# A two-layer decoder: order of the first loads and of the first values, and the place of the causal attention's first preparation

## The chip, the cores and the metric

The kernel runs on one core of one Trainium2 chip. The metric is device time in microseconds (us) of one execution, the median of several runs. Engines are named as in the profile: PE (TensorE matmul), PEld (TensorE weight load), DVE (VectorE), ACT (ScalarE), POOL (GpSimd) and SP (SyncE, which here issues most of the DMAs; ACT's queue issues a few).

## What is computed

A decoder of two layers on x of shape (4, 512, 256), everything in float32. Each of the six parts adds its result to x after a layer norm. Cut to what matters here:

```python
x = x + L0_attn(layernorm(x))     # 16 heads of 64, rope, kerple bias, a small network over heads
x = x + L0_xattn(layernorm(x), ctx_1024)
x = x + L0_ffn(layernorm(x))      # attention with 8 heads, 5 experts for values and outputs
x = x + L1_attn(layernorm(x))     # causal, 16 heads of 16, rope
x = x + L1_xattn(layernorm(x), ctx_1024, mask)
x = x + L1_ffn(layernorm(x))      # 32 routed experts and 2 shared ones

def L0_attn(x):                   # per batch
    q, k, v = split(x @ w_qkv); q, k = rope(q), rope(k)
    scores = q @ k.T / 8
    kerple = -softplus(log_p) * log1p(softplus(log_a) * distance)
    hidden = gelu(concat(scores, kerple, over heads) @ w1 + b1)
    scores = scores + kerple + hidden @ w2 + b2
    return softmax(causal(scores)) @ v @ w_o
```

The small network mixes the 16 heads at each pair of positions, so it needs all heads of a score block side by side.

## The kernel before

Partitions hold 128 tokens or 128 channels. x stays in SBUF for the whole kernel as 16 tiles of 128 tokens, four per batch (`TB` = 4, `NT` = 16).

**The first attention** (`l0_attn`) works on blocks (b, ib): batch b, 128 query rows ib, and the ib + 1 blocks of keys that the causal mask leaves. `turned(b, side, g)` projects a group of four heads of queries (side 0) or keys (side 1): it loads 256 KB of weights (tile `wqk`, three buffers), projects two halves on PE (L125), multiplies each with cosine and sine on DVE (L212, L213) into `rope_c` and `rope_s`, of one buffer each, and subtracts and adds on POOL (L214, L215) into `qk`. `scores(b, ib, g0, ng, on_act)` multiplies queries and keys of `ng` groups (L235), scales the result out of PSUM on ACT (L247, for the rows in `on_act`) or DVE (L245) into a ring `sc` of six buffers, and stores it from SP to DRAM (L248); the heads come to lie side by side there. `fetch(b, ib)` reads a block back as `st` (L260). Then for 16 groups of rows g: `hidden` (L269 on PE, L271 on DVE, gelu L272 on ACT, L273 on POOL) and `refined` (L281 on PE, L287 on DVE); and, for 16 groups, `weights` (the exponential, L301 on ACT), followed by the division. `values` projects one 128 x 512 piece of v (eight units per batch, PE L125, out by ACT L223).

Work of other blocks is put between these groups by hand: the list `beside(b, ib)` goes beside the network, `beside_weights(b, ib)` beside the exponentials; there about 70% of the list is placed and the rest (`left`) goes beside the first three groups of the next block. For block (0,0) `beside` holds the scores of (0,1) and (0,2), and `beside_weights` the values of batch 0 and the statistics of batch 1. The order of PE, ACT, DVE and POOL is the order of the program (`manual_schedule`); each is a queue, and an instruction that waits holds all behind it. SP's order is the scheduler's.

Ahead of that, before: x is loaded whole (2 MB) as the first load of SP's queue; `wv` and `wo` (1 MB each) go out on ACT's queue; SP loads `cs` (512 KB) and the small weights, then the distances. The kerple term `ker` is computed in a buffer of `rope_c`, so the norm, which writes `rope_c` too, comes after `hk`, the network's share of `ker` (L179, L180). Then follow the norm of batch 0, its transposes, all eight `turned`, all scores of block (0,0) in one call, and the fetch.

**The ffn of layer 0** (`l0_ffn`) walks 64 steps: step s handles pair of heads s mod 4 of token tile t = s // 4 with scores, row maximum and exponential (L1344, L1351, L1352), transposes (L1363), the output (L1380), and later `divide`, `weigh` (five products with the expert mask on POOL, L1408, in tile `mix`, three buffers), `total`, `experts` and `rows`, which add to x (L131). `at(step, f)` puts a call at a step. `spread(b)` puts the preparation of batch b beside batch b - 1; the last batch (steps 48 to 63) has nothing of that kind beside it.

**The causal attention** (`causal`, inside `l1_heads`) follows. For its first batch, before: weights and rope table are loaded, the norm is taken, four transposes (`tokens`), four projections (`turned`, two sides of two halves, L1121 on DVE), the sums on POOL and stores to a DRAM tile `way` (`store`, L1131, L1132), memsets of the padded buffers `m4`, `kT`, `qT`, `v` on POOL (`preset`, L790 to L795), and the reads of `way` back into `qT` and `kT` (`fetch`, L1138), all ahead of the first score matmul (L579); the value projections come at the first steps.

Of the kernel before, what the change touches and what calls it, by code (L numbers as in the profile page):

```python
# [134 lines left out]
def l0_attn(k, a):  # L135
# [7 lines left out]
    with ExitStack() as ctx:  # L143
# [7 lines left out]
        wv = load(k, wp, a, "l0a_wv", eng=nc.scalar)  # L151
        cs = load(k, wp, a, "l0a_cs")
        w1s, w1k, w2, b1, pab = (load(k, wp, a, "l0a_" + n) for n in ("w1s", "w1k", "w2", "b1", "pab"))
        wo = load(k, wp, a, "l0a_wo", eng=nc.scalar)


        sp = t_(wp, [P, 2], F32, "sp")
        nc.vector.tensor_scalar(sp, pab[:, 0:2], -1.0, None, ALU.mult)
        sq = t_(wp, [P, 2], F32, "sq")
        nc.vector.tensor_tensor(sq, sp, pab[:, 0:2], ALU.min)  # L160
        nc.scalar.activation(sq, sq, AF.Exp)
        nc.scalar.activation(sq, sq, AF.Ln, bias=k.one[:, 0:1])
        nc.vector.scalar_tensor_tensor(sp, pab[:, 0:2], 0.0, sq, ALU.max, ALU.add)
        ker = t_(work, [P, 2, S], F32, "rope_c", 1)[:, 0, :]
        nc.sync.dma_start(out=ker, in_=a["l0a_dist"])
        nc.scalar.activation(ker, ker, AF.Ln, bias=k.one[:, 0:1], scale=sp[:, 1:2])
        nc.vector.tensor_scalar(ker, ker, sp[:, 0:1], -1.0, ALU.mult, ALU.mult)

        kerm = t_(wp, [P, S], F32, "kerm")
        nc.vector.tensor_scalar(kerm, ker, pab[:, 2:3], None, ALU.add)  # L170
        ahead = t_(wp, [P, 8], F32, "ahead")
        nc.sync.dma_start(out=ahead, in_=a["l0a_ahead"])
        nc.vector.tensor_tensor(kerm[:, 504:512], kerm[:, 504:512], ahead, ALU.add)

        hk = t_(wp, [P, 2, S], F32, "hk")
        for half in range(2):
            rows = slice(half * 64, half * 64 + 64)
            ps = k.ps()
            nc.tensor.matmul(ps, lhsT=w1k[rows], rhs=ker[rows], start=True, stop=True)  # L179
            nc.scalar.activation(hk[:, half], ps, AF.Identity, bias=b1[:, 0:1])  # L180
# [230 lines left out]
        def beside(b, ib):  # L411

            if ib == 0:
                before = output_list(b - 1, 3)
                return before + (score_list(0, 1) + score_list(0, 2) if b == 0 else [])
            if ib == 1:
                return mixed(mixed(score_list(b, 3), output_list(b, 0)), norms.pop(b + 1, []))
            if ib == 2:
                return output_list(b, 1)
            out = output_list(b, 2)  # L420
            return out[:6] + score_list(b + 1, 0) + out[6:]

        def beside_weights(b, ib):

            if ib == 0:
                return mixed(value_list(b), norm_list(b + 1) if b + 1 < B else [])
# [3 lines left out]

        ET = mybir.EngineType
        with k.tc.manual_schedule(engines={ET.PE, ET.Activation, ET.DVE, ET.Pool}):
            for _, f in norm_list(0) + norms.pop(0) + turned_list(0, range(4)) + score_list(0, 0):
                f()
            fetch(0, 0)
            fill = []
# [409 lines left out]
def cross(k, a, pre, wp, work, bufs, preset, masked=None):  # L846
    nc = k.nc
    if True:
        rest = {}

        def fetch(*names):
            for n in names:
                if n == "keep_kT":
                    of = t_(wp, [P, 2560], F32, "held").bitcast(BF16)[:, : SC // P * S]
# [14 lines left out]
        def last():  # L869
            for n in ("wo", "bo") + ("bv",) * (masked is not None):  # L870
                rest[n] = load(k, wp, a, pre + n)
            rest["wv"] = load(k, wp, a, pre + "wv", tag="l1_wv" if masked else None)
# [10 lines left out]
        def prep(b, m):  # L883
# [8 lines left out]
            def turned(i):  # L892
                if i == 0:
                    xs["T"] = t_(work, [P, 2, S], F32, "xnT", 1)
# [35 lines left out]
            def queries(c, n):  # L930
                if n == c == 0:

                    xs["q"] = t_(work, [P, 2, S], F32, "ln_xn", 1)
# [16 lines left out]
            norm = fs(norm_units(k, work, b, xs, on_act=start), 0.4)  # L950
# [136 lines left out]

def causal(k, a, wp, work, bufs, preset):
    nc = k.nc
    if True:  # L1090
        wv = load(k, wp, a, "l1a_wv", tag="l1_wv")
        wo = load(k, wp, a, "l1a_wo")

        both = t_(wp, [P, 2560], F32, "held")
        wqk = both[:, :1024].rearrange("p (i s n) -> p i s n", i=2, s=2)
        tab = both[:, 1024:].rearrange("p (i n) -> p i n", i=3)
        nc.sync.dma_start(out=wqk, in_=a["l1a_wqk"])
        nc.sync.dma_start(out=tab, in_=a["l1a_tab"])

        def prep(b, m):  # L1100
            qT, kT, v = bufs[b % 2]
            xs = {}

            def tokens(i):
                if i == 0:
                    xs["T"] = t_(work, [P, 2, S], F32, "xnT", 1)
                transposed(k, xs["xn"], xs["T"], i)

            def turned(side, half):
                if half == 0:  # L1110

                    xs["s", side] = t_(work, [P, 2, 2, S], F32, ("stage", "cT")[side], 1)
                st = xs["s", side]
                ps = k.ps()
                proj(
                    k, ps, lambda i: wqk[:, i, side, half * P : (half + 1) * P],
                    lambda i: xs["T"][:, i, :],
                )

                for own, n in (0, 0), (1, 1 + half):  # L1120
                    nc.vector.scalar_tensor_tensor(  # L1121
                        st[:, own, half ^ own], ps, (0.25, 1.0)[side], tab[:, n], ALU.mult, ALU.mult
                    )

            def store(side):
                st = xs["s", side]
# [773 lines left out]
```

## Time and profile before

The median of three runs is 3678.42 us (3677.25 to 3681.02). The profile is of one more execution.

| | us |
|---|---|
| profiled execution, its time | 3683.43 |
| its span in the profile | 3681.7 |
| PE busy | 3418.3 |
| DVE busy | 2152.5 |
| ACT busy | 1536.3 |
| POOL busy | 941.9 |
| first statistics of x (L48) | at 11.22 |
| first rope product (L212) | at 28.96 |
| first network matmul of block (0,0) (L269) | at 79.97 |
| first network matmul of block (0,1) | at 125.39 |
| end of the ffn's last addition to x | at 1977.39 |
| first causal score matmul (L579) | at 2014.22 |

An engine's busy time is the sum over its instructions; a DMA that is issued is not counted for the issuing engine. The chain of waits is followed back from the last instruction: each row is what released the next. In rows by stretch the granted clock is the share of full speed at which PE was let run. Idle time on an engine that nobody waits for costs nothing, so the weak stretches of PE are what to look at, and in each the wait that ends last.

### The profile page before, as it was taken

To read this page: it belongs to the slowest core of one execution; us is meant where nothing else is said; L and a number is where in the kernel's file an instruction comes from. 1 tells how busy PE (TensorE), PEld (TensorE's weight loads), DVE (VectorE), ACT (ScalarE), POOL (GpSimd) and SP (SyncE) were. 2 spreads that over 40 slices of the span, in tenths; PEclk is the share of its full clock that TensorE was granted. 3 is DMA by queue.
4 is the path that set the end of the run, shared out by engine and by line. 5 is a ranking of instruction groups with operands and counts; after the bars stand their busy time and mean duration, and the time that the engine had idled before them with its cause. 6 is when DMAs were issued, how large, how long until landed. Compare 5 with 4: busy or idle time off the path is not lost.

```text
span 3681.7 us, 51748 instructions
## 1 busy us (share of the span) xinstructions
PE 3418.3 (93%) x19152; PEld 1591.2 (43%) x19152; DVE 2152.5 (58%) x4822; ACT 1536.3 (42%) x3329; POOL 941.9 (26%) x1167
## 2 busy tenths in 40 slices
PE   5999999997799999979995999999999999999999
PEld 3445454453443333345553444333333244444444
DVE  3575676755477666467783677888888622122211
ACT  1545555455445555634442344444445511111111
POOL 2342433423311012036673322000000012222222
PEclk8999999998899999979997899999999999999999
DMA  3423323141120111000002121010010032111111
GB/s 122 161 81 113 115 97 111 63 149 58 42 44 21 30 33 46 1 21 1 1 1 63 29 58 44 12 29 13 18 18 1 16 133 94 50 52 49 52 52 43
DMA packets 118877, 196.58 MB, mean 53 GB/s; under 512 B 12384, under 2 KB 62048, under 8 KB 116448
## 3 DMA queue, kind: packets, MB, share of 16 engines
q1 hardware_dynamic: 118080, 190.65, 17.1%
q8 instruction: 151, 2.47, 0.3%
q10 hardware_dynamic: 544, 2.62, 0.2%
q14 instruction: 102, 0.84, 0.1%
HBM read 128.74 MB, written 51.90 MB: 49 GB/s over the span
## 4 chain that ended last, share of the span: by engine, by line
PE 78%; DVE 9%; issue 4%; POOL 4%; ACT 2%; DMA 2%; SPq 0%; ACTq 0%; DVEq 0%; POOLq 0%
PE ps L572 15%; PE big L125 10%; PE ps L125 10%; PE av L647 8%; PE ps L579 6%; PE acc L1568 5%; PE hp L269 4%; PE ps L281 3%; PE ps L330 2%; PE ps L348 2%; PE ps L235 2%; PE ps L586 2%; PE ps L362 2%; DVE hd L271 1%; PE ps L1344 1%
## 5 line engine op out<-in xcount | busy, mean ns | idle before, releaser
L591 ACT ACTIVATE pT<-ps 128x512 f32<-128x512 f32 (+3 forms) x1280 | 649.9, 565 | 614.0 <-PE ps L579 335.3
L579 PE MATMUL ps<-kT,qT 32*128 32x512 f32 (+3 forms) x2560 | 791.3, 611 | 34.5 <-DMA kT<-way 20.9
L572 PE MATMUL ps<-q,kT 32*128 32x512 f32 (+3 forms) x2560 | 682.1, 606 | 0.7 <-DVE mx L615 0.6
L125 PE MATMUL big<-xnT,w 128*128 128x512 f32 x1088 | 492.5, 596 | 0.0
L1556 DVE TENSOR_TENSOR gu<-big,silu 128x512 f32<-128x512 f32 x136 | 94.0, 691 | 572.3 <-ACT silu L1554 572.1
L612 DVE TENSOR_REDUCE mx<-ps 128x1 f32<-128x512 f32 x512 | 326.6, 685 | 163.8 <-PE ps L579 163.6
L615 DVE CUSTOM_DVE_ANT_0 junk<-ps,mask_q 128x512 bf16<-128x512 f32 x512 | 353.0, 689 | 92.9 <-PE ps L572 25.6
L572 PEld LDWEIGHTS ps<-q,kT 32*128 32x128 f32 x2560 | 212.8, 183 | 337.8 <-ACT pT L591 117.9
L1554 ACT ACTIVATE silu<-big 128x512 f32<-128x512 f32 x136 | 81.2, 597 | 619.4 <-PE big L125 619.4
L647 PE MATMUL av<-pT,v 128*32 128x512 f32 (+3 forms) x2560 | 323.1, 574 | 0.5 <-ACT un L655 0.4
L125 PEld LDWEIGHTS big<-xnT,w 128*128 128x128 f32 x1088 | 208.1, 191 | 262.5 <-issue 262.5
L272 ACT ACTIVATE hd<-hd 128x16 f32<-128x16 f32 (+51 forms) x256 | 162.8, 636 | 351.9 <-DVE hd L271 351.8
L273 POOL TENSOR_TENSOR st<-st,kerm 128x8 f32<-128x8 f32 (+51 forms) x256 | 190.4, 745 | 460.6 <-PE hp L269 398.1
L579 PEld LDWEIGHTS ps<-kT,qT 32*128 32x128 f32 x2560 | 255.5, 185 | 118.4 <-issue 47.3
L1560 POOL TENSOR_TENSOR gu<-gu,cb 128x512 f32<-128x512 f32 x128 | 163.5, 1277 | 552.6 <-DVE gu L1556 508.1
L1568 PE MATMUL acc<-gu,w 128*128 128x512 f32 x544 | 257.9, 597 | 8.0 <-POOL gu L1560 8.0
L53 POOL TENSOR_TENSOR ln_rstd<-ln_rstd,mhalf 128x4 f32<-128x4 f32 x24 | 24.5, 1022 | 900.1 <-DVE ln_rstd L52 893.9
L269 PE MATMUL hp<-st,l0a_w1s 64*128 64x104 f32 (+26 forms) x1024 | 193.2, 455 | 55.3 <-DVE hd L271 46.2
L271 DVE TENSOR_TENSOR hd<-hp,hk 128x16 f32<-128x16 f32 (+51 forms) x256 | 178.4, 697 | 84.5 <-PE hp L269 78.5
L281 PE MATMUL ps<-hd,l0a_w 128*64 128x104 f32 (+26 forms) x1024 | 170.0, 411 | 32.2 <-ACT hd L272 25.9
L615 DVE CUSTOM_DVE_ANT_0 junk<-ps,ahead 128x256 bf16<-128x256 f32 (+3 forms) x256 | 125.5, 490 | 84.6 <-PE ps L579 58.4
L1352 ACT ACTIVATE pr<-ps,nmax 128x512 f32<-128x512 f32 x128 | 87.0, 686 | 192.3 <-DVE nmax L1351 192.1
(241 smaller groups left out, 4989.2 us busy)
## 6 DMA issues: line engine op xcount, KB each, us to landing
cb<-comb SPq DMA_DIRECT2D x128, 256.0 KB
scr<-sc SPq DMA_DIRECT2D x112, 256.0 KB
st<-scr SPq DMA_DIRECT2D x16, 1024.0 KB
w<-in_l1f_w SPq DMA_DIRECT2D x34, 384.0 KB
scr<-sc SPq DMA_DIRECT2D x64, 192.0 KB
st<-scr SPq DMA_DIRECT2D x16, 768.0 KB
wqk<-in_l0a_wqk SPq DMA_DIRECT2D x32, 256.0 KB
st<-scr SPq DMA_DIRECT2D x16, 512.0 KB
```

Source lines behind the costliest of these rows:

```text
L125: k.nc.tensor.matmul(out, lhsT=lhsT(c), rhs=rhs(c), start=start and c == 0, stop=stop and c == 1)
L269: nc.tensor.matmul(hp[:, half, :n], lhsT=w1s[rows], rhs=s[rows, :n], start=True, stop=True)
L271: nc.vector.tensor_tensor(hd[:, :, :n], hp[:, :, :n], hk[:, :, S - n :], ALU.add)
L273: nc.gpsimd.tensor_tensor(s[:, :n], s[:, :n], kerm[:, S - n :], ALU.add)
L281: nc.tensor.matmul(rp[half * 64 : half * 64 + 64, :n], lhsT=w2, rhs=hd[:, half, :n], start=True, stop=True,)
L572: nc.tensor.matmul(pa[h][:, :w], lhsT=kT[rows, c, kb * P : (kb + 1) * P], rhs=q2s[g][rows, q0:], start=True, stop=not on_pe(g, h), tile_po ...
L579: nc.tensor.matmul(pb[r][:, :uw], lhsT=uqT[rows, uc, qb * P : (qb + 1) * P], rhs=ukT[rows, uc, kh * 512 : kh * 512 + uw], start=True, stop ...
L591: nc.scalar.activation(pT[:, h, :w], pa[h][:, :w], AF.Exp)
L612: nc.vector.tensor_reduce(to, pb[r], AX.X, ALU.max)
L615: nc.vector.tensor_tensor_reduce(out=junk[:, :uw], in0=pb[r][:, :uw], in1=mask, scale=1.0, scalar=-3.0e38, op0=ALU.add, op1=ALU.max, accum ...
L647: nc.tensor.matmul(avs[g][h * 32 : h * 32 + 32, q0:], lhsT=v[:, kb, (c * 4 + h) * 32 : (c * 4 + h) * 32 + 32], rhs=pT[:, h, : S - q0], sta ...
L1568: nc.tensor.matmul(accs[b][:, n, :], lhsT=w[e][:, 512 + n * P : 512 + (n + 1) * P], rhs=g, start=e == experts[0], stop=e == experts[-1],)
```

## The change

**Loads.** x is loaded in two pieces, batch 0 first on SP, the rest later on ACT's queue. `pab`, the distances, `w1k` and `b1` go on ACT's queue at the start, `cs`, `w1s`, `w2` and `ahead` on SP's. `wv` is loaded on ACT's queue after the fifth and sixth `turned`, x's rest and `wo` after the last scores of block (0,0).

**Front.** `ker` has a buffer of the ring `sc`. The norm and the transposes come first, then `from_kerple` (the same instructions as before, in a function), then the eight `turned` in four pairs, `made_of_kerple` after the first, and the scores of block (0,0) one group of heads at a time, one pair behind, each evicted by ACT alone (16 stores in place of 4). The eight value units of batch 0 come right after the fetch of block (0,0). The scores of (0,2) leave the list beside the network of block (0,0) and take the place of the values beside its exponentials.

**Joint.** A pool `pre` is open over the ffn and layer 1. A class `Rotated` holds the causal part's first loads, norm, transposes, projections and stores. `l0_ffn` calls it at step 44 and puts the norm at steps 48 to 52, transposes at 54 and 55, queries at 57 to 59, keys at 60 to 62, the staging in two buffers of `mix`; here the norm is on DVE and not on ACT. For batch 0 `causal` keeps the memsets, the reads of `way` and the values, in this order, ahead of the first scores. In `weigh` of the last two tiles two of the five products go to DVE.

```diff
-        wv = load(k, wp, a, "l0a_wv", eng=nc.scalar)
-        cs = load(k, wp, a, "l0a_cs")
-        w1s, w1k, w2, b1, pab = (load(k, wp, a, "l0a_" + n) for n in ("w1s", "w1k", "w2", "b1", "pab"))
-        wo = load(k, wp, a, "l0a_wo", eng=nc.scalar)
...
-        ker = t_(work, [P, 2, S], F32, "rope_c", 1)[:, 0, :]
-        nc.sync.dma_start(out=ker, in_=a["l0a_dist"])
...
+        ker = t_(work, [P, S], F32, "sc", 6)
+        pab = load(k, wp, a, "l0a_pab", eng=nc.scalar)
+        nc.scalar.dma_start(out=ker, in_=a["l0a_dist"])
+        w1k, b1 = (load(k, wp, a, "l0a_" + n, eng=nc.scalar) for n in ("w1k", "b1"))
+        cs, w1s, w2, ahead = (load(k, wp, a, "l0a_" + n) for n in ("cs", "w1s", "w2", "ahead"))
+        wv, wo = (t_(wp, a["l0a_" + n].shape, F32, "l0a_" + n) for n in ("wv", "wo"))
...
             if ib == 0:
-                before = output_list(b - 1, 3)
-                return before + (score_list(0, 1) + score_list(0, 2) if b == 0 else [])
+                return output_list(b - 1, 3) if b else score_list(0, 1)
...
             if ib == 0:
-                return mixed(value_list(b), norm_list(b + 1) if b + 1 < B else [])
+                there = value_list(b) if b else score_list(0, 2)
+                return mixed(there, norm_list(b + 1) if b + 1 < B else [])
...
-            for _, f in norm_list(0) + norms.pop(0) + turned_list(0, range(4)) + score_list(0, 0):
+            for _, f in norm_list(0) + norms.pop(0):
                 f()
+            from_kerple()
+            for g in range(5):
+                if g < 4:
+                    for _, f in turned_list(0, (g,)):
+                        f()
+                if g == 0:
+                    made_of_kerple()
+                if g == 2:
+                    nc.scalar.dma_start(out=wv, in_=a["l0a_wv"])
+                if g:
+                    scores(0, 0, g - 1, 1, (0, 1, 2, 3))
+            nc.scalar.dma_start(out=k.x[:, TB:], in_=a["x"][:, TB:])
+            nc.scalar.dma_start(out=wo, in_=a["l0a_wo"])
             fetch(0, 0)
+            for _, f in value_list(0):
+                f()
...
+class Rotated:
+    def __init__(self, k, a):
...
+        self.wv = load(k, k.pre, a, "l1a_wv", tag="l1_wv")
...
+        nc.sync.dma_start(out=self.wqk, in_=a["l1a_wqk"])
+        nc.sync.dma_start(out=self.tab, in_=a["l1a_tab"])
+    def units(self, b, stage):
...
+        norm = norm_units(k, k.pre, b, xs)
+        return norm, [lambda i=i: tokens(i) for i in range(TB)], sides
...
             if b == 0:
                 chains = [
-                    (0, 0, norm + turns + fs([lambda: preset(0, 0, S)]) + sides + got),
-                    (0, 2, vs),
+                    (0, 0, fs([lambda: preset(0, 0, S)]) + got + vs),
...
             for e in range(FE):
-                nc.gpsimd.tensor_tensor(
+                eng = nc.vector if t >= NT - 2 and e % 2 else nc.gpsimd
+                eng.tensor_tensor(
...
+            def ahead():
+                k.rotated = Rotated(k, a)
+                norm, turns, sides = k.rotated.units(
+                    0, lambda side: t_(work, [P, 2560], F32, "mix", 3)[:, : 4 * S].rearrange(
+                        "p (o h n) -> p o h n", o=2, h=2
+                    ),
+                )
+                for i, u in enumerate(norm):
+                    at(n - 16 + i // 2, u)
+                for i, u in enumerate(turns):
+                    at(n - 10 + i // 2, u)
+                for i, u in enumerate(sides[0]):
+                    at(n - 7 + i, u)
+                for i, u in enumerate(sides[1]):
+                    at(n - 4 + i, u)
+            at(n - 20, ahead)
...
-        nc.sync.dma_start(out=k.x, in_=a["x"])
+        nc.sync.dma_start(out=k.x[:, 0:TB], in_=a["x"][:, 0:TB])
```

The functions `tokens`, `turned` and `store` are moved from `causal` into `Rotated` unchanged but for the tile that they stage in, which the caller gives. The second cross-attention takes some tiles from `pre` too, with the same instructions.

## The prediction, made before the changed kernel was run

> **What bounds the kernel now.** I read the page first (section 1, then the 40 slices), then the busy time by stretch around the two weak slices, then the chain of waits there, and last the rows in order of time.
>
> ```profile
> span 3681.7 us, 51748 instructions
> PE 3418.3 (93%) x19152; PEld 1591.2 (43%) x19152; DVE 2152.5 (58%) x4822; ACT 1536.3 (42%) x3329; POOL 941.9 (26%) x1167
> PE   5999999997799999979995999999999999999999
> PEclk8999999998899999979997899999999999999999
> ```
>
> PE is busy nearly everywhere, so a cut pays only where PE starves: slice 0 (0 to 92 us) and the two slices around 2000 us. The diff works at exactly these two places. I call them the front and the joint.
>
> ```profile
> 25.00:70.00 45.00, 35.08 (x120) 16.86 (x120) 19.97 (x32) 0.20 (x1) 19.77 (x16) 0.88 0.15 47
> 70.00:80.00 10.00, 0.84 (x10) 0.55 (x10) 1.29 (x2) 2.37 (x3) 0.12 (x1) 0.50 0.51 155
> 80.00:116.60 36.60, 29.25 (x256) 18.50 (x256) 13.64 (x59) 11.22 (x29) 6.07 (x23) 0.72 0.62 206
> 116.60:125.40 8.80, 8.80 (x23) 3.73 (x22) 3.11 (x15) 8.24 (x35) 1.82 (x12) 1.00 0.13 47
> ...
> 1900.00:1954.00 54.00, 53.56 (x465) 35.93 (x464) 39.37 (x63) 35.27 (x93) 18.43 (x18) 1.00 0.00 1
> 1954.00:1977.00 23.00, 12.53 (x84) 8.21 (x82) 7.35 (x12) 3.79 (x11) 10.24 (x10) 0.79 0.00 1
> 1977.00:2014.20 37.20, 11.03 (x24) 4.78 (x25) 7.87 (x19) 3.23 (x8) 15.88 (x15) 0.64 0.46 116
> ```
>
> Columns: stretch, length, busy time of PE, weight load, DVE, ACT, POOL, granted clock, DMA share, GB/s. Front: rope (25 to 70), a wait of 10 us for scores to go to DRAM and back, then block (0,0): its network (80 to 116.6) and its weights (to 125.4). Joint: the ffn's last batch fills PE; its tail leaves PE half idle; then 37.2 us pass before the first causal score.
>
> ```profile
> 42.22 1.26 POOL qk L214
> 43.48 1.23 POOL qk L215
> 44.71 0.02 issue
> 44.74 0.69 DVE rope_c L212
> ...
> 77.11 2.81 DMA st<-scr
> ...
> 98.14 5.69 DMA scr<-sc
> ...
> 116.68 8.78 PE ps L125 x20
> ```
> ```profile
> 1964.15 5.12 POOL mix L1408 x5
> ...
> 1984.43 8.88 PE ps L125 x16
> ...
> 1997.20 9.53 DMA way<-cT
> ...
> 2008.09 6.00 DMA kT<-way
> ```
>
> Chain rows are start, length, what. Rope is a serial loop of DVE and POOL over one pair of buffers: the DVE rows start every 5.08 us (39.66, 44.74, 49.82), eight times. PE only follows.
>
> **Front, term by term.** *Start.* Before, the first stats wait for all of x (11.22), SP's queue then stands until 15.25 behind the big loads, and DVE's norm comes after the kerple work (22.36); rope begins at 28.96. After, a quarter of x comes first. No row shows a 512 KB load alone. The third wqk load (256 KB) lands 3.5 us after its issue (16.58 to 20.09) and the other 256 KB cost 0.8 us at 322 GB/s, the mean of the first 16 us; with the 0.80 of the issue and some company (dist, cs) I take 5.5. Bounds: 4.5, and 11.2 if the order changes nothing. From there: stats and root 3.5 (11.22 to 14.75), norm, transposes and four copies 2.9. ACT then does the kerple chain that DVE's queue now has before the first rope product: two table loads of 1.28, Exp 0.2, Ln 0.29 and 0.81, and on DVE 0.16 + 0.48 + 0.48 + 0.17: 5.2. Rope starts at 17.1. The projections are ready earlier (5.5 + 3.5 + 2.9 + 3.7 cold = 15.6), so kerple decides. **-11.8.**
>
> *Rope.* Still 8 x 5.08. The 16 scores evictions are all on ACT, idle there (0.20 us busy), so DVE loses nothing. SP issues 16 stores in place of 4, some 0.6 each, and a wqk load queued behind four of them (2.4 us) lands late for its projection twice or so: **+1.5** (0 to 4).
>
> *Gap.* From the last POOL row (70.12) to the first network matmul (79.97) PE waits 9.85. The eight value units, 32 matmul instructions at 8.78/20 = 14.0, now stand there, behind 1.6 of scores: 15.8, **+6.0**. They cover the wait for st. But x's rest and wo, 2.5 MB, start on ACT's queue just then, beside the last store and 1 MB of st: 3.75 MB at 297 GB/s (the first 20 us) is 12.6, plus about 3 to start and land: level with the values. Bounds: +5 and +11.
>
> Here a rule speaks against the change: the Trainium skill, DMA: Bandwidth & Descriptors, "Issuing engines are not separate DMA queues", says that transfers from any issuing engine share 16 DMA engines and interleave. The trace agrees at the start, where x, 2 MB, needs 10.4 us beside 2 MB on ACT's queue. If st had priority the gap would be +6.0, and by the rule it is +6 to +8.
>
> *Network of block (0,0).* Four calls of scores(0,2) leave it: on the chain 2.80 + 2.87 + 2.87 and the 5.69 of waiting for an sc buffer, so 36.3 - 14.2 = 22.1. From below: 16 steps of about 1.2 (0.9 at 80.92, 1.5 at 91.22) and two calls of scores(0,1) at 2.4: 24. I take 24: **-12.3** (22 to 30).
>
> The same stretch ran at a granted clock of 0.72. The skill's TensorE: Matmul & The Clock Gate, Part 1, gives half rate after an idle window of about 3.4 us and full rate after a busy one; the 0.50 in the gap agrees. By it the values keep PE warm and 29.25 us of PE work would shrink by up to 8; my 24 uses rows that are partly warm, so the sum has some of that.
>
> *Weights of block (0,0).* Values (8.78) leave, but ACT set that stage's length (8.24 of 8.80), so nothing is saved. Three of the four scores(0,2) calls come in: 2.3 MB through six sc buffers, while DVE and ACT, in order, hold weights and divisions behind a full ring. At 206 GB/s (80 to 116.6) that is 11.4; with a table load 13: **+3.9** (0 to +9). *Opening of (0,1).* Three value units leave (3 x 1.91), one scores call stays: **-3** (-4 to +3).
>
> Front: -11.8 + 1.5 + 6.0 - 12.3 + 3.9 - 3 = **-15.7**.
>
> **Joint.** *Weigh.* POOL's five products take 5.12, twice on the chain (1954.20, 1964.15). Three stay on POOL (3.07), two go beside them to DVE (0.69 each): 2 x 2.05 = **-4.1** (0 if POOL and DVE slow each other, -4.1).
>
> *Work moved into the last batch.* PE: 16 projection instructions at 0.43 (their spacing from 29 to 50 us) = 6.9, transposes 8 x 0.14 (1.09 for eight of L1363) = 1.1, so 8.0. PE has no slack (53.56 of 54), so it all counts. DVE gets 4 x 0.57 + 0.17 + 4 x 0.35 + 8 x 0.65 = 9.1 on 39.4 of 54; POOL 1.0 + 5.0 on 18.4; ACT four copies. Their cover is their slack; scores wait for DVE's maximum, so some shows: **+9.5** (0 to 20). SP is idle in the ffn, so the loads and the four stores delay nobody. The stores' 9.5 us end before the ring gives their mix buffer to weigh, five steps (17 us) on. The new pool only moves tiles to other addresses: nothing.
>
> *Gap.* What remains after the ffn's last matmul: m4, kT and qT memsets 0.99 + 1.81 + 1.80 on POOL, then eight fetches on SP (1.74 + 2.51), the last landing 6.0 after its issue: 4.6 + 3.7 + 6.0 = 14.3 in place of 37.2: **-22.9**. Before, the first load there is issued at 1977.01, at the end of the ffn's last matmul, so I let the memsets wait for it; if they need not, the gap is about 6 (-31); if the fetches collide with mask loads, 19 (-18). Values run in that wait and no longer between the first scores: 3.13 + 1.99, part of it then idle anyway: **-2** (-4 to 0).
>
> Joint: -4.1 + 9.5 - 22.9 - 2 = **-19.5**.
>
> **Sum.** -35. The profiled execution took 3683.4 (span 3681.7), 0.14% over the median of 3678.4; the same cut from the median gives **3643** (3648 for a profiled execution).
>
> **Rivals.** *The front gives most of it back* (0.17): scores(0,2) are bound by stores wherever they stand. For: 5.69 on the chain, 0.62 DMA share. Against: 8.8 us at a share of 0.13 just after. Network 30, weights 18, start as summed: -11.8 + 1.5 + 8 - 6.3 + 9 + 3 = +3.4, so 3678 - 19.5 + 3 = 3662. *The last batch pays double* (0.09), +20: 3654. *Memsets are not held* (0.08): 3643 - 8 = 3635. *It doesn't do what it says* (0.02): x's quarter lands no earlier, as the queues share engines: +5.7, 3649. *Slower* (0.03): the adds put DVE and POOL in front of scores, max and Exp in each of the last 16 steps, so the batch runs at the pace of the earlier ones, which carry the next batch's preparation and take 96.0 (POOL 63, DVE 74 busy). With 8.0 of PE and 5.0 of POOL adds on top: 109 for 54, +55 in place of +9.5: 3678 - 44.7 + 55 = 3689. It decides once that batch passes 54 + 44.7 = 98.7. Against: the earlier batches' POOL has 28 us of products, the moved work 6.
>
> **How the numbers follow.** Forecast 0.61, 3632 to 3655 on its own. The range 3626 to 3664 takes in all but the ends of the first rival and the slower one; front bounds of some 10 each way and joint bounds of some 11 add to about 15 when independent, a little more on the late side. A measurement of this kernel can tell about 0.2%, or 7 us: faster 0.94, same 0.03, slower 0.03.
>
> **What would show it.** First stats near 5.5, rope's first product near 17, its last POOL row near 60, first network matmul near 75 with 14 us of value projections before it, and block (0,1)'s first near 110 (125.4 before). Last batch's 54 at 62 to 65; weigh at 3.1 on POOL twice; first causal score some 14 after the ffn's last matmul and about 35 earlier in all than 2014. It is wrong if waits on sc fill the weights stage, if projections wait in the rope for wqk, or if PE idles in the last batch.

## The result and the profile after

The changed kernel takes 3660.07 us (median, 3658.52 to 3660.62) against 3679.51 us (3677.25 to 3681.02) for the kernel before on the same chip: a ratio of 0.9947, 95% interval 0.9930 to 0.9964, so 19.4 us less. The direction was as forecast and the time lies inside the range; the size was too large by 17 us (3643): the time lies outside the main forecast's own range (3632 to 3655, chance 0.61) and near the 3662 of its first rival. The two profiled executions, which the sum was made on, took 3683.43 and 3658.52: 24.9 us less, where the terms said 35.2.

The page of the changed kernel, its first lines and two of its rows of 40 slices:

```profile
span 3656.8 us, 51742 instructions
PE 3419.3 (94%) x19089; PEld 1595.7 (44%) x19152; DVE 2156.1 (59%) x4827; ACT 1537.0 (42%) x3339; POOL 940.2 (26%) x1163
PE   7899899997799999979997999999999999999999
PEclk8899999998899999989997899999999999999999
```

PE's busy time did not fall (3419.3 against 3418.3, with 63 matmul records missing here; the same kernel run again, with all records, has 3426.8), so all of the gain is PE idle time that went. Slice 0 rose from 5 to 7 tenths. By stretch, with the same columns as before (stretch, length, PE, weight load, DVE, ACT, POOL, granted clock, DMA share, GB/s):

```profile
25.00:58.30 33.30, 23.52 (x97) 10.48 (x95) 14.99 (x24) 2.36 (x12) 16.36 (x14) 0.85 0.34 103
58.30:74.40 16.10, 16.09 (x42) 7.10 (x42) 0.00 (x0) 4.89 (x11) 0.00 (x0) 0.89 0.70 234
74.40:100.20 25.80, 21.87 (x191) 15.45 (x190) 10.38 (x51) 9.07 (x23) 5.80 (x21) 0.67 0.27 89
100.20:106.00 5.80, 4.19 (x38) 2.06 (x39) 3.21 (x12) 5.79 (x27) 1.86 (x12) 1.00 0.49 157
106.00:126.50 20.50, 15.61 (x82) 7.46 (x82) 9.97 (x34) 9.85 (x30) 3.28 (x10) 0.67 0.66 231
1890.00:1946.30 56.30, 56.30 (x437) 35.36 (x435) 41.26 (x67) 31.71 (x85) 21.47 (x20) 1.00 0.05 13
1946.30:1969.80 23.50, 14.90 (x107) 10.12 (x101) 13.95 (x20) 6.01 (x16) 7.98 (x6) 0.86 0.05 18
1969.80:1984.50 14.70, 5.24 (x17) 4.10 (x17) 0.41 (x1) 1.49 (x4) 9.91 (x10) 0.73 0.73 98
```

The gap after the rope is full of values (16.09 of 16.10), the network of block (0,0) takes 25.8 in place of 36.3, and the joint's empty stretch 14.7 in place of 37.2. The stretch that did not shrink is 106 to 126.5, the opening of block (0,1): PE works 15.6 of 20.5, and at a clock of 0.67.

The start, in DVE's rows in order of time (start, length, line, operation; in brackets the idle time before and what ended it):

```profile
5.91 0.43 DVE L48 BATCH_NORM_STATS2 ln_st<-x 128x6 f32<-128x256 f32 x1 [5.91 <-DMA x<-in_x]
...
16.22 0.17 DVE L421 TENSOR_TENSOR kerm<-kerm,l0a_ahead 128x8 f32<-128x8 f32 x1
16.30 0.69 DVE L191 TENSOR_TENSOR rope_c<-ps,l0a_cs 128x512 f32<-128x512 f32 x1
```

The quarter of x lands at 5.91 (11.22 before), and the kerple chain is what the first rope product waits for, as worked out: 16.30 in place of 28.96. At the joint, the chain of waits (start, length, what):

```profile
1958.10 4.00 POOL mix L1449 x3
...
1966.53 3.24 PE ps L1477 x6
1969.77 0.03 POOLq L804
1969.80 0.07 issue
1969.87 0.99 POOL m L804 x2
1970.86 1.74 POOL kT L805
1972.60 1.76 POOL qT L807
...
1977.42 6.87 DMA kT<-way
1984.29 0.20 issue
1984.48 4.55 PE ps L593 x15
```

The memsets (L804 to L807) start when the ffn's last matmul ends, then come the fetches, whose last transfer takes 6.87; the first causal score stands at 1984.48. Nothing of the norm, the projections, or the store to `way` is left in the chain.

To place gains and losses, it helps to have marks that every kernel here has: the start of POOL's reciprocal root (L53) of each layer norm. Five of them are used below: batch 1's norm in the first attention, the last norm of the ffn, the second and the third of the causal attention, and the time from its third to its fourth.

| | batch 1 | ffn, last | causal, 2nd | causal, 3rd | 3rd to 4th | end (span) |
|---|---|---|---|---|---|---|
| before | 127.1 | 1814.3 | 2028.6 | 2065.8 | 73.9 | 3681.7 |
| after | 116.8 | 1799.6 | 1995.4 | 2034.0 | 80.9 | 3656.8 |
| difference | -10.3 | -14.7 | -33.2 | -31.8 | +7.0 | -24.9 |

So the change was ahead by 31.8 at the third causal norm, and 7 us of that were lost in the next 81 us, in code that the diff does not touch. The windows there, of before, then of after:

```profile
2066.00:2084.00 18.00, 16.23 (x89) 7.33 (x89) 9.55 (x38) 6.07 (x14) 4.02 (x9) 0.99 0.22 39
2084.00:2094.00 10.00, 10.00 (x52) 5.33 (x52) 4.13 (x16) 3.06 (x11) 0.81 (x2) 0.51 0.00 1
2094.00:2140.00 46.00, 45.61 (x352) 22.06 (x344) 33.94 (x118) 21.56 (x55) 14.06 (x27) 1.00 0.19 47
```
```profile
2034.00:2042.00 8.00, 6.72 (x43) 3.56 (x44) 5.95 (x25) 2.19 (x6) 2.58 (x5) 0.98 0.49 85
2042.00:2068.00 26.00, 24.78 (x86) 9.98 (x84) 6.68 (x25) 6.59 (x17) 2.44 (x6) 0.50 0.00 1
2068.00:2115.00 47.00, 46.80 (x361) 22.76 (x360) 34.84 (x121) 21.92 (x56) 13.88 (x27) 0.99 0.20 46
```

Both run a while at a granted clock of one half there: 10 us before, 26 after.

The marks scatter between executions of the same code. Eight profiles, this one and seven of the runs below, have the same front (the changed kernel twice, e1, e7 to e10 and e12): batch 1's norm lies at 116.3 to 118.4 in them. Six of these (all but e1 and e9) have the same code up to the ffn's last batch as well: its last norm lies at 1797.4 to 1804.2. The way from the first causal norm, the one that the change moved into the ffn, to the second is steadier: 101.4 to 101.6 in the eight profiles that have this part unchanged.

### The profile page after: what moved, and what is told of

Read it like the earlier page. It is cut to its first block, busy times and chain, and to the rows that moved or that the text cites. A ratio compares the mean times of both kernels' runs of the same rounds, so it can differ in the third digit from the quotient of the medians.

```text
span 3656.8 us, 51742 instructions
## 1 busy us (share of the span) xinstructions
PE 3419.3 (94%) x19089; PEld 1595.7 (44%) x19152; DVE 2156.1 (59%) x4827; ACT 1537.0 (42%) x3339; POOL 940.2 (26%) x1163
## 5 line engine op out<-in xcount | busy, mean ns | idle before, releaser
L629 DVE CUSTOM_DVE_ANT_0 junk<-ps,mask_q 128x512 bf16<-128x512 f32 x512 | 352.6, 689 | 92.5 <-PE ps L586 25.8
L251 ACT ACTIVATE hd<-hd 128x16 f32<-128x16 f32 (+51 forms) x256 | 162.7, 636 | 344.0 <-DVE hd L250 343.9
L53 POOL TENSOR_TENSOR ln_rstd<-ln_rstd,mhalf 128x4 f32<-128x4 f32 x24 | 24.5, 1023 | 875.2 <-DVE ln_rstd L52 750.8
```

The lines of the kernel that those rows point to most:

```text
L629: nc.vector.tensor_tensor_reduce(out=junk[:, :uw], in0=pb[r][:, :uw], in1=mask, scale=1.0, scalar=-3.0e38, op0=ALU.add, op1=ALU.max, accum ...
```

## The experiments

All were timed beside the kernel before; the ratio is of mean times and so not quite that of the medians. "Whole" is the changed kernel. Edits are shown against it.

| run | median us | ratio, 95% interval | batch 1 | ffn, last | causal, 2nd | causal, 3rd | 3rd to 4th |
|---|---|---|---|---|---|---|---|
| e0_whole | 3657.03 | 0.9925 (0.9909 to 0.9941) | 116.3 | 1797.4 | 1993.2 | 2031.8 | 80.9 |
| e1_front | 3674.03 | 0.9968 (0.9955 to 0.9981) | 117.2 | 1802.5 | 2019.5 | 2056.8 | 80.9 |
| e2_joint | 3672.79 | 0.9970 (0.9954 to 0.9986) | 129.6 | 1812.0 | 2009.0 | 2047.8 | 79.4 |
| e3_s02_back | 3656.48 | 0.9929 (0.9911 to 0.9947) | 120.0 | 1800.9 | 1996.7 | 2035.5 | 73.9 |
| e5_loads_early | 3661.87 | 0.9940 (0.9924 to 0.9956) | 116.8 | 1803.2 | 1998.9 | 2037.5 | 80.9 |
| e6_split | 3646.48 | 0.9901 (0.9881 to 0.9921) | 112.4 | 1792.0 | 1987.8 | 2026.5 | 73.9 |
| e11_split_again | 3646.39 | 0.9902 (0.9886 to 0.9918) | 111.8 | 1791.5 | 1987.2 | 2026.1 | 73.9 |
| e7_vs_late | 3665.43 | 0.9953 (0.9936 to 0.9971) | 118.4 | 1804.2 | 2004.0 | 2041.9 | 79.4 |
| e8_weigh_pool | 3664.58 | 0.9942 (0.9925 to 0.9959) | 116.6 | 1797.7 | 1995.6 | 2034.7 | 79.3 |
| e9_earlier | 3668.11 | 0.9951 (0.9936 to 0.9965) | 117.7 | 1816.2 | 2009.2 | 2048.9 | 76.5 |
| e10_full_rows | 3668.00 | 0.9958 (0.9944 to 0.9972) | 117.8 | 1801.1 | 1996.8 | 2035.5 | 80.9 |
| e12_full_rows_there | 3667.84 | 0.9954 (0.9938 to 0.9970) | 116.5 | 1802.9 | 1998.7 | 2037.3 | 85.5 |

### The whole change, and each half alone

e0 is the changed kernel with no edit.

> The changed kernel once more, beside its parts. Main theory: 19 us faster than before (0.9947), give or take 2. The stretch of half clock in the first causal blocks (25 us in the first profile of the change, 9.5 us in that of before) depends on where the work falls on the clock's windows, so a second profile of the same kernel may show another length. Rival (the stretch belongs to the new order of the causal start): 25 us again, in each kernel that has the new joint and in no other.

It took 25.4 us less than before in this call (3657.03 against 3682.42), where the first comparison had 19.4; the two intervals overlap. Single executions of one kernel spread over 12 to 16 us in this call: 3653.97 to 3665.67 for the whole, 3678.90 to 3695.09 before. The stretch after the third causal norm was the long one again (80.9). e1 keeps the front alone:

```diff
-            at(n - 20, ahead)
...
-                    (0, 0, fs([lambda: preset(0, 0, S)]) + got + vs),
+                    (0, 0, norm + turns + fs([lambda: preset(0, 0, S)]) + sides + got),
+                    (0, 2, vs),
...
-                eng = nc.vector if t >= NT - 2 and e % 2 else nc.gpsimd
+                eng = nc.gpsimd
```

> The front alone, joint as before. Main theory: the rope's first product at 16.3 and the first network matmul at 74.4 as in the whole change, block (0,1)'s transposes 11 us earlier than before, and 11 us kept to the ffn; total -11 (0.9970). Rival (front and joint are not independent; the front's gain decays or grows downstream): total below -5 or above -16.

And e2 keeps the joint alone:

```diff
-            from_kerple()
-            for g in range(5):
...
-            for _, f in value_list(0):
-                f()
+            for _, f in norm_list(0) + norms.pop(0) + turned_list(0, range(4)) + score_list(0, 0):
+                f()
```

> The joint alone, front as before. Main theory: first causal score 17 us earlier than before, the last batch of the ffn about 10 us longer, the gap 14.7 in place of 37.3; total -8 to -17, by how long the half clock lasts in the first causal blocks (9.5 us: -17; 25 us: -10). Rival (the new causal start causes the long stretch of half clock): 25 us of half clock and -10 or less.

By the ratios the front alone is worth 12 us (7 to 17), the joint alone 11 (5 to 17) and the whole 28 (22 to 34): the halves add up within these intervals, which are too wide to size a term. The marks do better: in e1 the front puts batch 1's norm 9.9 us earlier and the last norm of the ffn 11.8 (8.7 to 10.8, and 10.1 to 16.8, in the profiles of the same code against the one of before); the joint shortens the way from there to the third causal norm from 251.5 (before) and 254.3 (e1) to 235.8 (e2) and 234.4 (whole): 16 to 20 us, where the prediction had 19.5. So the joint paid about in full, and the front, at batch 1's norm, less than its 15.7.

The long stretch at half clock is in e1 too, with the causal start as before and in its old order (columns as above):

```profile
2056.00:2066.00 10.00, 8.60 (x56) 4.08 (x56) 6.66 (x28) 2.85 (x8) 2.98 (x6) 0.92 0.41 79
2066.00:2092.00 26.00, 24.77 (x96) 10.55 (x96) 7.95 (x28) 6.90 (x19) 2.03 (x5) 0.51 0.00 0
2092.00:2138.00 46.00, 45.60 (x353) 21.97 (x345) 33.94 (x118) 21.60 (x55) 14.08 (x27) 1.00 0.20 47
```

So the theory that the new causal start makes those 7 us falls: they come with the old one too, and are absent in e3, which has the new one.

### Where scores(0,2) stand

e3 puts the scores of block (0,2) back beside the network of block (0,0) and leaves the values where the change has them.

```diff
-                return output_list(b - 1, 3) if b else score_list(0, 1)
+                return output_list(b - 1, 3) if b else score_list(0, 1) + score_list(0, 2)
...
-                there = value_list(b) if b else score_list(0, 2)
+                there = value_list(b) if b else []
```

> The whole change, but the scores of (0,2) stand beside the network of (0,0) again, as before; values stay in the gap. Main theory: the stall on the score ring in the exponentials of (0,0) (4.8 us on ACT, 6.5 on DVE) goes, the network of (0,0) grows from 25.8 to some 37, and the front ends level: total within 3 us of the whole change. If scores(0,2) beside the exponentials were a clear gain, as the prediction had it (-12.3 + 3.9 - 3), this is 10 us slower than the whole change.

The network of block (0,0), to the start of its last matmul, took 39.0 us (74.5 to 113.5) in place of 25.8, so the calls cost 13.2 there, near the 12.3 of the prediction. But from there to the transposes of block (0,1) (L309) only 16.8 passed (to 130.3) and not 26.4: beside the exponentials and in the opening, the same calls cost 9.6. The move is worth 3.6 us, at batch 1's norm too (120.0 against 116.3 in e0). The totals do not show it (3656.48 against 3657.03), as e3's profile has the short stretch after the third causal norm. Why it costs so much there is in the rows of the changed kernel, of ACT and then of PE:

```profile
111.28 0.49 ACT L226 ACTIVATE sc<-ps 128x384 f32<-128x384 f32 x1 [4.78 <-DMA scr<-sc]
```
```profile
106.33 3.15 PE L214 MATMUL ps<-qk 32*128 32x384 f32 x16
113.69 0.85 PE L248 MATMUL hp<-st,l0a_w1s 64*128 64x144 f32 x4 [4.20 <-DVE hd L250]
```

ACT stands 4.78 us for a buffer of the ring `sc` whose store has not left (DVE, for its eviction, 6.5), and the last exponentials queue behind it. The second hidden matmul of (0,1), which needs DVE past these, comes 13.5 us after the network's last matmul starts (100.15 to 113.69). In e3, with no scores beside the exponentials, it comes 5.8 us after (113.52 to 119.31): 7.7 of the 9.6. The clock of this stage does not tell the two apart. The stage in the whole (e0), then in e3:

```profile
100.30:126.70 26.40, 21.31 (x118) 10.01 (x118) 13.17 (x48) 15.81 (x55) 5.17 (x21) 0.67 0.62 213
```
```profile
113.50:130.30 16.80, 9.30 (x55) 4.35 (x55) 9.66 (x38) 12.40 (x47) 4.83 (x18) 0.70 0.16 57
```

### The loads in the gap, and a version that is faster

e5 issues the rest of x and `wo` between the `turned` calls, with `wv` one pair earlier.

```diff
-                if g == 2:
+                if g == 1:
                     nc.scalar.dma_start(out=wv, in_=a["l0a_wv"])
+                if g == 2:
+                    nc.scalar.dma_start(out=k.x[:, TB:], in_=a["x"][:, TB:])
+                if g == 3:
+                    nc.scalar.dma_start(out=wo, in_=a["l0a_wo"])
...
-            nc.scalar.dma_start(out=k.x[:, TB:], in_=a["x"][:, TB:])
-            nc.scalar.dma_start(out=wo, in_=a["l0a_wo"])
```

> The whole change, but wv, x's rest and wo go out one pair of projections apart inside the rope and not after it. It measures what the 2.5 MB cost beside the last score store and the st read. Main theory: they delay st (issued at 70.0 in the whole change, 8.5 us after the last store; some 3 us after it here, so at 64 to 65), but 15 us of values stand ahead of the network anyway, so the first network matmul stays at 74.4 within 1 us and the total within 2 of the whole change. Rival: the wqk loads are held up in their place, and the rope ends 2 to 6 us later.

SyncE's issue of the fetch of `st` (L239), which waits for the last stores of the scores; the changed kernel first, then e5:

```profile
70.00 2.03 SPq L239 DMA_DIRECT2D st<-scr  x4
```
```profile
62.76 2.03 SPq L239 DMA_DIRECT2D st<-scr  x4
```

The fetch leaves 7.2 us sooner, and the first network matmul is still at 74.4 in both, since the values run to that moment: the loads beside the stores cost 7 us that the values hid. The rope's last product row ends at 58.15 (58.26 in the changed kernel), so the rival falls. The time is that of the whole within the intervals (3661.87). That agrees with the Trainium skill, DMA: Bandwidth & Descriptors, "Issuing engines are not separate DMA queues": the loads on ACT's queue and the stores on SP's share the engines.

With that, the values in the gap are longer than the wait that they fill. e6 adds to e5: five of the eight value units in the gap, three beside the exponentials, and half of scores(0,2) beside the network.

```diff
-                return output_list(b - 1, 3) if b else score_list(0, 1)
+                return output_list(b - 1, 3) if b else score_list(0, 1) + score_list(0, 2)[:2]
...
-                there = value_list(b) if b else score_list(0, 2)
+                there = value_list(b) if b else mixed(vals[5:], score_list(0, 2)[2:])
...
-            for _, f in value_list(0):
+            vals = value_list(0)
+            for _, f in vals[:5]:
```

> Loads early as in e5, and the fill of block (0,0) spread: five values in the gap, three beside the exponentials; two calls of scores(0,2) beside the network, two beside the exponentials. If the price of the change's own layout is the score ring (2.3 MB through six buffers beside the exponentials) and values beyond the gap, the first network matmul comes at about 69, and batch 1's norm 3 to 6 us earlier than in the whole change (116.5). Rival (PE at half clock or DMA rate sets block (0,0), wherever the pieces stand): within 1.5 us of 116.5.

It takes 3646.48, and 3646.39 when run again (below): 0.990 of before, ahead of both kernels; e5, in the same call, took 3661.87. The network of block (0,0) in e6, then the exponentials and the opening of (0,1), up to the transposes:

```profile
70.40:101.70 31.30, 21.49 (x221) 14.64 (x220) 11.92 (x55) 10.87 (x27) 5.73 (x21) 0.84 0.54 183
101.70:119.70 18.00, 17.25 (x99) 7.70 (x99) 11.13 (x44) 15.42 (x54) 5.18 (x21) 0.90 0.35 127
```

The network starts at 70.4 in place of 74.4 and is longer (31.3 against 26.0 in e0); a full ring still holds ACT for 4.16 us and DVE for 4.57 in it. The second stage is shorter by more: 18.0 in place of 26.4, with PE busy for 17.25 of it. Transposes of block (0,1): 119.7 against 126.7. Batch 1's norm is 3.9 us earlier than in e0 and the third causal norm 5.3.

> The kernel of e6_split once more, with no change: to tell what of its gain is its front and what the clock of one stretch. If the front is the gain: batch 1's norm near 112 us again and a median of 3643 to 3651 whichever length the stretch after the third causal norm has. If the clock made it: 3652 to 3658 where that stretch is long (80.9 us between the third and the fourth causal norm).

e11 is that kernel with no edit. Batch 1's norm came at 111.8 and the median at 3646.39, as in e6. But its stretch after the third causal norm was short again (73.9), so the run does not separate the front's 4 to 6 us (against e0) from the 7 us of that stretch; both are in the 10.5 to 13.7 us that lie between these medians and the whole's two.

### Where the causal values stand

```diff
-                    (0, 0, fs([lambda: preset(0, 0, S)]) + got + vs),
+                    (0, 0, fs([lambda: preset(0, 0, S)]) + got),
+                    (0, 2, vs),
```

> The whole change, with the causal values of batch 0 back between the first score matmuls and not ahead of them in the wait for the reads. The prediction's term (-2): the second causal norm comes 2 us later (0 to 4) against the sixth ffn landmark and the total is 0 to 4 us slower than the whole change. Rival: PE has nothing in the wait, the clock goes to half before the first scores, and they cost 5 to 8 us more.

From the first causal norm (1898.4 here, 1891.7 in e0) to the second 105.6 us passed, in place of 101.5: the values in the wait for the reads are worth 4.1 us up to there (3.3 up to the third norm), at the far end of the -2 (-4 to 0) of the prediction and short of the rival's 5 to 8.

### The split of the products

```diff
-                eng = nc.vector if t >= NT - 2 and e % 2 else nc.gpsimd
+                eng = nc.gpsimd
```

> The whole change, but all five products of weigh on POOL in the last two tiles too. By the prediction's term 4.1 us are lost between the last batch and the first causal score (POOL 5.12 in place of 3.07, twice). By the rows of the whole change (3.99 with DVE beside it) 2.3 are lost. If the tail is held by something else, nothing.

From the moved norm (1891.9) to the second causal norm: 103.7 in place of 101.5, so the split is worth 2.2 us and not 4.1, as the expectation's second reading had it (2.3). The groups of line 1449 in the changed kernel, 1920 to 1990 us (out<-in, count | busy, mean ns | idle before):

```profile
L1449 POOL TENSOR_TENSOR mix<-o,sel 128x512 f32<-128x512 f32 x11 | 13.1, 1220 | 13.1 <-issue 10.7 <-DVE o L1436 2.3
L1449 DVE TENSOR_TENSOR mix<-o,sel 128x512 f32<-128x512 f32 x4 | 4.3, 1119 | 0.1
```

Three products on POOL take 4.00 (1.33 each) beside two on DVE, where five alone take 5.13 in e8 (1.03 each): 30% slower. DVE's take 1.12; the prediction's 0.69 was from another line, with one input in PSUM. The bound of that term was nothing, "if POOL and DVE slow each other", and they do. The Trainium skill has the rule that was not weighed: GPSIMD Engine Reference, "1. Specifications", has POOL's way into SBUF shared with DVE, with contention when a DVE instruction has two SBUF inputs, as these have.

### The same work in an earlier batch

e9 puts batch 0's causal norm, transposes and projections some twenty steps earlier (from step 28, its norm at 1787.9), into batches that still prepare the next one.

```diff
-                    at(n - 16 + i // 2, u)
+                    at(n - 36 + i // 2, u)
...
-                    at(n - 10 + i // 2, u)
+                    at(n - 32 + i // 2, u)
...
-                    at(n - 7 + i, u)
+                    at(n - 31 + i, u)
...
-                    at(n - 4 + i, u)
+                    at(n - 28 + i, u)
...
-            at(n - 20, ahead)
+            at(n - 38, ahead)
```

> The whole change, but causal batch 0's norm, transposes and projections stand at steps 28 to 38 of the ffn, where PE has 7 to 9 us idle per batch of 95, and not at 48 to 62, where it has none. If the 9.8 us that the last batch grew by are PE time, they go away: first causal score 6 to 10 us earlier than in the whole change, the third batch longer by 0 to 4. Rival (DVE and POOL, in order, set the earlier batches): the third batch grows by 8 or more, and nothing is gained.

In e0 PE is idle for 9 and 7 us in the two intervals between norms there (busy 85.35 of 94.30 and 87.16 of 94.20), so the 8.0 us of PE work might have hidden. They did not: from the norm of the ffn's third batch to the second causal norm e9 takes 301.4 us (1707.8 to 2009.2), the whole 290.0 (1703.2 to 1993.2), and the ffn's last norm came at 1816.2. POOL and DVE carry a whole preparation there already (63 and 74 us busy of 94), which is what the rival named; what held PE in e9 was not traced further, so that cause is argued and not shown.

### The half clock after the third causal norm

Two runs put extra matmuls of 128 rows into the causal scores, to see whether the gate falls because the score matmuls use 32 rows each.

```diff
+        if t and this.causal and g in (7, 8):
+            nc.tensor.matmul(
+                pa[heads[0]][:, : min(w, 256)], lhsT=k.ident, rhs=k.x[:, NT - 1, : min(w, 256)],
+                start=True, stop=True,
+            )
```

> The whole change, and in the causal scores of two groups of heads (about 2034 to 2070 us) one extra matmul of 128 rows x 256 columns ahead of each call's score matmuls, into the same PSUM tile, which the score matmul then overwrites: some 16 to 32 of 0.35 us at full clock, 6 to 11 us of PE work added. Theory A, the clock gate counts how much of the array works, not whether a matmul is in flight, and the score matmuls with 32 rows in use and few per microsecond let it fall to half: then the full-row matmuls hold it up, the stretch at 0.50 there (25 us in the profile of the changed kernel) is gone or under 5 us, and the third causal norm stands 68 to 76 us before the fourth (80.9 in the changed kernel, 73.9 where the stretch was short), the total 5 us faster to level. Theory B, it is phase alone, and the extra matmuls do nothing to the clock: 80 to 92 us between these norms and the total 6 to 11 us slower.

> As e10_full_rows, but in the two groups of heads that do run in the stretch (in e10 the extra matmuls stood some 70 us later, behind the stretch, where 28 of 0.31 us made the time between the fourth and the fifth causal norm 50.0 us in place of 45.7: +4.3 is their price at full clock). Theory A, the gate counts work in the array: the clock stays up or comes back within 10 us, 70 to 79 us between the third and the fourth causal norm (80.9 without them), total level with the whole change or up to 6 us faster. Theory B, phase alone or a gate that these do not reach: the long stretch at 0.50 stays, and 28 more matmuls at half clock make it 85 to 92 us, the total 4 to 11 us slower than the whole change.

e12 has groups 4 and 5 for 7 and 8. Both miss their place, e12 too, against what its expectation says. The summary of the extra line in e12 (count, shortest, median and longest ns, first and last start):

```profile
L584 PE MATMUL ps<-x,ident x32: 273/380/484, 2091.7 to 2126.6; 128*128 128x256 f32 x24, 128*128 128x128 f32 x8
```

Its half clock was over by 2074, ahead of the first of them. So neither run tests theory A. What they give: 32 such matmuls cost some 4.5 us (85.5 against 80.9 in e12; 50.0 against 45.7 in the next interval in e10), and the long stretch stands in two more profiles, of the whole's code up to there.

Over all profiles but that of e12 the interval is 73.9 in before, e3, e6 and e11, 76.5 in e9, 79.3 to 79.4 in e2, e7 and e8, and 80.9 in after, e0, e1, e5 and e10. It was the same in both profiles of the two kernels that have two (whole, split), which is too few to say that it belongs to a kernel: the executions of one kernel lie up to 19 us apart (e6, 3642.53 to 3661.23), and only one of a set is profiled. It goes neither with the joint's order (e1, e3) nor with the absolute time (long and short both at a third norm of 2035.5, e10 and e3). What sets it stays open.

## Why the prediction was right, and where its size was off

The terms against the rows, on the two profiled executions:

| step | forecast | measured | from |
|---|---|---|---|
| start | -11.8 | -12.7 | first rope product 28.96 to 16.30 |
| rope | +1.5 | +0.8 | last product row, 70.12 to 58.25 |
| gap | +6.0 | +6.3 | 9.85 to 16.12 |
| network of (0,0) | -12.3 | -10.5 | 36.3 to 25.8 |
| weights of (0,0), opening of (0,1) | +0.9 | +5.3 | 21.1 to 26.4 |
| from the transposes of (0,1) to the ffn's last norm | 0 | -3.9 | -10.8 to -14.7 |
| weigh and moved work | +5.4 | +7.5 | last ffn matmul 1976.95 to 1969.77, less -14.7 |
| joint's gap | -22.9 | -22.6 | 37.3 to 14.7 |
| causal values | -2 | -2.0 | first causal score to third norm, 51.6 to 49.6 |
| half clock after the third causal norm | 0 | +7.0 | 73.9 to 80.9 |
| sum | -35.2 | -24.8 | |

**Right:** that the change pays only at the two places where PE starves; that the kerple work, not the projections, decides the rope's start; that the values cover the wait for `st`, loads included (e5); that the memsets are held by the ffn's last matmul, so that rival falls; that x's quarter comes early (so the change does what it says); that the last batch takes the moved work once and not twice: from the ffn's last norm to its last matmul 170.2 us in place of 162.7, which with the 2.2 of the split is 9.7 for the moved work (9.5 forecast). The slower rival, which needed +44.7 there, was far off.

**Right by luck: rope.** The +1.5 stood for `wqk` loads that come late behind the stores, and the rope did lose 0.8. But no load is late in it: DVE waits 2.74 and 1.09 us for PE (at 36.77 and 39.15), PE's row before that waits for DVE (its load was issued at 20.38, 12.5 us earlier), and then PE runs at a clock of 0.50. PE's row, and the stretch:

```profile
32.90 9.65 PE L125 MATMUL ps<-xnT,wqk 128*128 128x512 f32 x16 [3.18 <-DVE rope_s L192]
```
```profile
31.20:38.00 6.80, 5.10 (x6) 2.19 (x7) 3.71 (x6) 0.00 (x0) 2.81 (x3) 0.50 0.54 183
```

**Not as reasoned: network.** It came near its -12.3 (-10.5), but not by a warm PE: its clock was 0.67, below the 0.72 of before, in spite of 16 us of values just ahead of it.

**Mis-sized: weights and opening of block (0,0).** "+3.9 (0 to +9)" and "-3 (-4 to +3)" came to +5.3 together. The first rival, that the front gives most of it back, described this place rightly: three scores calls through six buffers put DVE's and ACT's in-order queues behind a full ring. It came in part, and the time is near that rival's 3662 by luck, as its front was to be 3.4 us slower than before and block (0,1) is 10.8 earlier: the network kept its 10.5, while e3 shows 9.6 of the 13.2 us that the calls cost in the network spent again behind it. The step that failed is pricing the calls by their bytes at a mean rate (2.3 MB at 206 GB/s, 11.4 us) and then letting the opening gain 3 us: the ring held ACT for 4.78 us and DVE for 6.49, and the opening's own work behind them. The clock of this stage fell too (1.00 before, from 116.2 to 137.4; 0.74 after), which the sum did not have; but e3, without the calls, has 0.70 there and is 9.6 us shorter, so the clock alone does not make the loss. e6, with two of the calls back beside the network and three value units beside the exponentials, takes 18.0 us for this stage.

**Mis-sized: weigh.** Forecast -4.1, measured -2.2 (e8), as POOL and DVE slow each other.

**Not in the sum: the clock.** The 7 us after the third causal norm are code that the diff does not touch, at 0.50 for 26 us in place of 10. Without them the profiled execution would have been 3651.5, within 4 us of the 3648 that the prediction gave for one. That closeness is partly luck, as the -3.9 between block (0,1) and the joint is in no term either and hides most of the front's miss: 3 of it lie between the ffn's second and third norm, 100.8 us in the profile of before and 97.4 to 99.0 in all others, e2 with the old front among them (99.0). From batch 1's norm to the ffn's last, six profiles of the same code scatter by 5 us (1681.1 to 1686.4; 1687.2 before), so whether it belongs to the change is open.

The rest of the 17 us between the predicted median and the measured one: the terms are off by 10.3, the two profiles lie 3.9 above (before) and 1.6 below (after) the medians of their kernels, and the median of before moved by 1.1.

## What to carry to other kernels

Work that is moved out of a stage must be priced where it lands by the queue that it enters there, not by its bytes: a ring that runs full holds two in-order engines, and all that waits behind them. When filler covers a wait, measure the wait without it: here the filler hid 7 us of slow loads, and with these loads moved it could shrink, which is part of the best version (3646 us). Splitting elementwise work over two engines can gain less than the count says: here five products split 3 to 2 over POOL and DVE gave 2.2 us, not 4.1.

## What was not expected of the hardware

- The granted clock stayed at 0.50 for 26 us while PE's records show it busy for 24.78 of them, with 86 matmul records, 46 of them of 32 rows. The Trainium skill, TensorE: Matmul & The Clock Gate, Part 1, has full rate return after a busy window of about 3.4 us; read by the records, these 26 us hold several and it did not. Here busy records alone do not tell when the clock rises (the profile models where a matmul ends); what does is open.
- The 16 us of back-to-back values before the network did not carry the clock through it: 0.67 over 74.4 to 100.2.
- Kernels with the same joint, which differ in the order of the first 130 us alone, take 73.9 (e3, e6) or 80.9 us (whole, e5) in the same causal code 2 ms later. Whole and e6 gave the same length again in a second profile; two profiles each do not show that it belongs to the kernel.
